# ScalarE's copy of U2 first in its pair, scaling of result rows in the pair's second place, result chunks made of runs of 32 elements

## The chip, the cores and the metric

The kernel runs on one core of a Trainium2 chip. A core has five engines that work side by side, each through its own instructions in order: TensorE (PE in the profile, its weight loads PEld), VectorE (DVE), ScalarE (ACT), GpSimd (POOL) and SyncE (SP, which here only issues transfers). They wait for one another through semaphores. SBUF is the working memory of 128 partitions, PSUM the memory into which TensorE writes and from which DVE and ACT read. The metric is the device time of one execution in microseconds (us), the median of several.

## What is computed

A block of attention, then a mixture of experts over 4096 tokens of 512 numbers:

```python
x = x + jnp.tanh(g_xattn[0]) * _L0_xattn_ref(_layernorm(x), ctx_1024, ctx_1024, ...)
x = x + jnp.tanh(g_ffn[0]) * _L0_ffn_ref(_layernorm(x), Wr, br, W1, b1, W2, b2)

# _L0_ffn_ref: 8 experts, 2 per token, each expert takes at most 615 rows
xg = x[disp_tok].reshape(E, cap, Dm)
h = jax.nn.silu(jnp.einsum('ecd,edh->ech', xg, W1) + b1[:, None, :])
out = jnp.einsum('ech,ehd->ecd', h, W2) + b2[:, None, :]
gated = out * disp_g.reshape(E, cap, 1)
y = jnp.zeros((N, Dm), x.dtype).at[disp_tok].add(gated.reshape(E * cap, Dm))
```

Each expert gathers its rows, multiplies them by W1 (512 x 2048), applies SiLU, multiplies by W2 (2048 x 512), scales each row by its gate and adds it to its token's row. All of it is in 32-bit floats.

## The kernel before

The first half of the time is attention, which the change doesn't touch. The experts follow one after another, with 616 columns (rows of the expert) in two halves of 308. Features lie on partitions: `xg_t` holds an expert's inputs, `o_t` its results, each as four chunks of 128 features.

**Products.** Both multiplications use Winograd's form of Strassen's scheme, with seven products in place of eight. `up(e, i)` (L912) computes pair i of an expert: hidden chunks i and i + 8 for both halves of the columns, 8 pairs per expert. Its products are of two matmuls each, and each matmul shows as two rows in the profile, so a product is four rows. In PE's order they are: P1, P2, U2 (added onto P1 in PSUM), P5, U3 (again onto P1), P3, and a last one onto P1. Between them stand small instructions: ACT copies P1 (`p1s`, L927), DVE adds it to P2 (`c11`, L930) and ACT applies SiLU (result "11", L931, recorded at L923); ACT copies U2 (L947), DVE adds P5 to it (`v`, L951); ACT copies U3 (L954), DVE makes c22 (L956), ACT SiLU "22"; DVE makes c12 (L961), ACT SiLU "12"; at last ACT applies SiLU "21" to PSUM itself. Since U3 is added onto the PSUM tile that holds U2, its matmuls wait for the copy of U2. `down` (L973) does the same for W2 in two long passes of eight matmuls a product.

**Weight and h sums.** The scheme needs sums of blocks. `sum_w1(e, i)` makes those of W1 on POOL, four instructions of 256 elements (L612 to L615). `sum_h(e, i)` makes those of the hidden results on DVE, four instructions of 308 elements (L880 to L883), each with two inputs in SBUF.

**What hangs on the pairs.** The order of all work is written out by hand. `up` calls `hook(1)` after SiLU "11" and `hook(3)` after SiLU "12"; `in_up` (L1124) says what they emit. At place 1 these are: in expert 0's pairs 2, 4 and 6 a step of the routing of later experts (`route_on`); the h sums of the pair before; the load of W1 three pairs ahead (SP); the weight sums of the next pair (POOL); from expert 1 on, in pairs 1 to 5, `put_laid` for a row chunk of the expert before, and in pairs 0 to 4 `lay_out` for one. At place 3 there is a routing step. A routing step is a string of small DVE instructions (L658 to L781) with a short matmul, or the gathers of an expert (L792, POOL).

**How results leave.** An expert's results are features by rows in `o_t` and must become rows. `lay_out(e, s)` (L827) transposes 32 x 32 blocks of a chunk of 128 rows on DVE into a tile `laid` (L832, or four pieces at L836 for the last chunk), and four transfers on SP (L840) bring its 32-partition pieces into a tile `eo` of 128 rows. `put_laid` (L856) scales the rows by their gates on ACT (L859) and issues, on POOL, an indirect transfer that adds the rows to the output (L1061). Three `eo` tiles take turns. Only the last expert's results go another way: `put_rows` (L1043) turns them on PE, scales them on ACT from PSUM (L1050) and scatters them.

**Layout of a row.** The weights come rearranged from the host (`chunks`, L1197): chunk c holds features 4 p + c on its partition p, for W1's inputs and for W2's outputs. So `lay_out` and `put_rows` put the four chunks side by side, element by element: a chunk's elements are written 16 bytes apart.

```python
# L830, lay_out; L1051, put_rows
to = t.rearrange("p (q i c) -> p q c i", q=DC, c=DC)
eo[:m, :].rearrange("p (i c) -> p c i", c=DC),
```

Of the kernel before, what the change touches and what calls it, by code (L numbers as in the profile page):

```python
# [17 lines left out]
P = 128  # L18
# [3 lines left out]
DC = D // P  # L22
TT = S // P
NT = B * TT
E, HID = 8, 2048
# [4 lines left out]
NST = 5  # L30
COLS = [min(P, C2 - s * P) for s in range(NST)]
BL = 32
# [12 lines left out]
def gated_block(ctx: ExitStack, tc: tile.TileContext, a: dict, out: bass.AP):  # L45
# [127 lines left out]
    with ExitStack() as at:  # L173
# [265 lines left out]
        for b in range(B):  # L439
            for c in range(DC):  # L440
                t = c * TT
# [36 lines left out]
        with tc.manual_schedule():  # L478
# [45 lines left out]
            for n, u in enumerate(units):  # L524
                b, c, qc = u
# [275 lines left out]

    laid, rows_out = {}, {}

    def lay_in(e, s):
# [20 lines left out]
    def lay_out(e, s):  # L827

        t = ex.tile([P, D], F32, tag="laid", name="laid", bufs=3)
        to = t.rearrange("p (q i c) -> p q c i", q=DC, c=DC)  # L830
        if LB[s] == BL:
            nc.vector.transpose(to, o_t[e][:, :, s * P : (s + 1) * P].rearrange("p c (q j) -> p q c j", q=DC))  # L832
        else:
            for q in range(DC):
                j0 = s * P + q * LB[s]
                nc.vector.transpose(to[:, q], o_t[e][:, :, j0 : j0 + BL])  # L836
        m = ROWS[s]
        rows_out[e, s] = ex.tile([P, D], F32, tag="eo", name="eo", bufs=3)
        for g in range(DC):
            nc.sync.dma_start(  # L840
                out=rows_out[e, s][:m, g * P : (g + 1) * P], in_=t[g * BL : g * BL + m // DC, :]
            )
# [13 lines left out]
    def put_laid(e, s):  # L856
        m = ROWS[s]
        eo = rows_out.pop((e, s))
        nc.scalar.activation(eo[:m, :], eo[:m, :], AF.Copy, scale=gates[e][:m, s : s + 1])  # L859
        put(e, s, eo, slots[:, e, :])  # L860
# [51 lines left out]
    def up(e, i, hook):  # L912

        w, s, x = w1.pop((e, i)), s1w.pop((e, i)), xg_t[e]
        k0, k1 = range(2), range(2, 4)
        if i == 0:
            h[e] = {}
        hh = h[e]

        def silu(q, g, src):  # L920
            hh[q, i] = ex.tile([P, CH], F32, tag=f"h{q}_{i}", name=f"h{q}_{i}")
            j = e * HC + i + g * NP
            nc.scalar.activation(hh[q, i], src, AF.Silu, bias=b1[:, j : j + 1])  # L923

        p1 = product([w[:, k, 0, :] for k in k0], [x[:, k, lhalf] for k in k0])
        p1s = temp("p1s")
        nc.scalar.copy(p1s, p1)  # L927
        p2 = product([w[:, k, 0, :] for k in k1], [x[:, k, lhalf] for k in k1])
        c11 = temp("c", 3)
        tt(c11, p2, p1s, ALU.add)  # L930
        silu("11", 0, c11)  # L931
        hook(1)
        first = e == 0 and i == 0

        def third():
            return product([s[:, 2, k, :] for k in k0], [x[:, k, rhalf] for k in k1])

        def fifth():
            return product([s[:, 0, k, :] for k in k0], [t[:, 0, k, :] for k in k0])

        t = tg[e]
        if first:

            p3, p5 = third(), fifth()
        product([s[:, 1, k, :] for k in k0], [t[:, 1, k, :] for k in k0], p1)
        u2 = temp("u2")
        nc.scalar.copy(u2, p1)  # L947
        if not first:
            p5 = fifth()
        v = temp("u4")  # L950
        tt(v, p5, u2, ALU.add)  # L951
        product([w[:, k, 1, :] for k in k0], [x[:, k, rhalf] for k in k0], p1)
        u3 = temp("u3")
        nc.scalar.copy(u3, p1)  # L954
        c22 = temp("c", 3)
        tt(c22, p5, u3, ALU.add)  # L956
        silu("22", 1, c22)
        if not first:
            p3 = third()
        c12 = temp("c", 3)  # L960
        tt(c12, p3, v, ALU.add)  # L961
        silu("12", 0, c12)
        hook(3)
        product([w[:, k, 1, :] for k in k1], [t[:, 2, k, :] for k in k0], p1)
        silu("21", 1, p1)
# [77 lines left out]
    def put_rows(e, s):  # L1043

        m = ROWS[s]
        pt = ps_x.tile([P, D], F32, tag="x", name="pt_o")
        for c in range(DC):
            nc.tensor.transpose(pt[:m, c * P : (c + 1) * P], o_t[e][:, c, s * P : s * P + m], ident)
        eo = ex.tile([P, D], F32, tag="eo", name="eo", bufs=3)
        nc.scalar.activation(  # L1050
            eo[:m, :].rearrange("p (i c) -> p c i", c=DC),  # L1051
            pt[:m, :].rearrange("p (c i) -> p c i", c=DC),
            AF.Copy,
            scale=last_gates[:m, s : s + 1],
        )
        put(e, s, eo, last_slots)
# [17 lines left out]
    with tc.manual_schedule():  # L1074
        load_w1(0, 0)
        load_w1(0, 1)
        for k, g in ((0, 1), (1, 1), (0, 0), (1, 0)):
            load_w2(0, 0, k, g, 1 + g)
        load_w1(0, 2)
        ex = ctx.enter_context(tc.tile_pool(name="ex", bufs=1))  # L1080
        candidates(0)
        for _ in range(BITS // LEVEL):
            narrow(0)
        above(0)
        places(0)
        one_hot(0, 0)
        for g in range(4):
            if g < 3:
                one_hot(0, g + 1)
            slot_tokens(0, g)  # L1090
        gather(0)

        idle = ps_h.tile([P, P], F32, tag="ps", name="idle")

        def busy(n):
            for _ in range(n):
                nc.tensor.matmul(idle, lhsT=ident, rhs=ident, start=True, stop=True)  # L1097

        busy(20)
        sum_w1(0, 0)  # L1100
        for s in range(3):
            turn(0, s)
            busy(4)

        def routing(e):

            yield lambda: candidates(e)
            for _ in range(BITS // LEVEL - 1):
                yield lambda: narrow(e)
            yield lambda: (narrow(e), above(e))  # L1110
            yield lambda: places(e)
            for g in range(4):
                yield lambda g=g: (one_hot(e, g), g and slot_tokens(e, g - 1))
            yield lambda: (slot_tokens(e, 3), gather(e))

        left = [step for e in range(1, E) for step in routing(e)]

        def route_on():
            if left:
                left.pop(0)()  # L1120

        for e in range(E):

            def in_up(i, n):  # L1124

                if n == 3:
                    if e == 0 or i > 1:
                        route_on()
                    return
                if e == 0 and i in (2, 4, 6):  # L1130
                    route_on()
                if i and i < NP:
                    sum_h(e, i - 1)
                if i + 3 < NP:
                    load_w1(e, i + 3)
                if 0 < i < NP - 1:
                    sum_w1(e, i + 1)
                if e:
                    if 0 < i <= NST:
                        put_laid(e - 1, i - 1)  # L1140
                    if i < NST:
                        lay_out(e - 1, i)
                if e == 0 and i == 0:

                    turn(0, 3)
                    turn(0, 4)
                    sum_x(0)
                    sum_w1(0, 1)
                if e == 0 and i == 5:
                    sum_w2(0, 0)  # L1150
                if e == E - 1 and i == NP - 1:
                    in_order(e)

            def in_down(m, n):
                if e == E - 1 and m == 1:
                    return
                if m == 0 and (n >= 0 if n % 1 == 0 else e == 0 and n < 0) or m == 1 and n in range(5):
                    route_on()
                if n % 1:
                    return  # L1160
                if m == 0 and n == 0:
                    sum_h(e, NP - 1)
                if e + 1 < E:
                    if m == 0 and n in (2, 4, 6):
                        load_w1(e + 1, n // 2 - 1)
                    if m == 0 and n == 6:
                        for s in range(3):
                            lay_in(e + 1, s)
                    if m == 1:
                        for s in ((0, 1), (2,), (3, 4), (), (), (), ())[n]:  # L1170
                            turn_laid(e + 1, s)
                        if n == 0:
                            lay_in(e + 1, 3)
                            lay_in(e + 1, 4)
                        if n == 3:
                            sum_x(e + 1)
                        if n in (1, 3):
                            sum_w1(e + 1, n // 2)

            for i in range(NP):  # L1180
                up(e, i, lambda n: in_up(i, n))
            for m in range(2):
                right_half = down(e, m, lambda n: in_down(m, n))
# [47 lines left out]
```

## Time and profile before

| What | us |
|---|---|
| median of 3 runs (2112.34 to 2114.98) | 2112.52 |
| the profiled execution | 2110.61 |
| its span, first to last instruction | 2108.5 |
| PE busy | 1999.0 (95%) |
| DVE busy | 1272.9 (60%) |
| ACT busy | 849.6 (40%) |
| POOL busy | 588.1 (28%) |
| attention, about | 0 to 1060 |
| experts, from expert 0's first product to the last product | 1120.6 to 2091.7 |

The granted TensorE clock is 0.986 on the mean. In the expert stage PE is busy for 98% of the time, DVE about 60%, ACT a quarter, POOL half; the transfers take up to half of the DMA engines' time.

How to read it: a row of a group gives line, engine, operation, the tiles written and read, their shape and the count; after the first bar the busy time in us and the mean of one in ns; after the second bar how long the engine had stood idle just before such instructions, and what ended that. A row of the timeline gives start and duration in us, then engine, line and operation; "x8" is eight rows of the same kind merged, and square brackets name an idle time before it. Matmuls are pipelined, so the end of one overlaps the start of the next; the pace of PE is read from starts. Waits of some 0.1 to 0.2 us are often not listed as waits, and are seen only in starts.

### The profile page before, as it was taken

How to read it: one execution, taken by the hardware profiler on the slowest of the kernel's cores; microseconds unless marked ns; L12 is line 12 of the kernel's file. 1: busy time of each engine (PE TensorE's matmuls, PEld its weight loads, DVE VectorE, ACT ScalarE, POOL GpSimd, SP SyncE). 2: the span in 40 equal slices, each digit the busy share in tenths (PEclk: the TensorE clock that was granted, in tenths of full speed). 3: DMA queues.
4: the chain of work that ended last, by engine and by line, in shares of the span. 5: the costliest groups of instructions: out<-in, count | busy, mean ns of one | idle time of the engine just before them, and what ended most of it. 6: DMA issues, size and time to landing. Idle time of an engine off the chain costs nothing.

```text
span 2108.5 us, 27762 instructions
## 1 busy us (share of the span) xinstructions
PE 1999.0 (95%) x9808; PEld 1237.5 (59%) x9808; DVE 1272.9 (60%) x2694; ACT 849.6 (40%) x2014; POOL 588.1 (28%) x800
## 2 busy tenths in 40 slices
PE   8999999999999999999749999999999999999997
PEld 3445555555555555555427667767777676767775
DVE  4566666566665666656576667676667667662430
ACT  3555556565555565655502214041322314042331
POOL 1001101010100001010104373554636354464623
PEclk9999999999999999999969999999999999999998
DMA  6010111002011010000042254555443444544431
GB/s 220 1 56 16 51 41 54 33 21 75 21 56 37 25 65 21 32 29 36 26 122 77 59 126 94 140 109 141 93 126 94 110 110 104 150 101 121 96 71 25
DMA packets 216938, 157.46 MB, mean 75 GB/s; under 512 B 17568, under 2 KB 186208, under 8 KB 216800
## 3 DMA queue, kind: packets, MB, share of 16 engines
q1 hardware_dynamic: 207968, 134.81, 21.7%
q0 software_dynamic: 8832, 20.88, 5.6%
q8 instruction: 78, 1.28, 0.3%
q14 instruction: 60, 0.49, 0.1%
HBM read 107.75 MB, written 29.77 MB: 65 GB/s over the span
## 4 chain that ended last, share of the span: by engine, by line
PE 89%; ACT 4%; DVE 3%; issue 2%; DMA 1%; POOL 0%; SPq 0%; POOLq 0%; DVEq 0%; ACTq 0%
PE ps L899 44%; PE pj L299 20%; PE pt L235 11%; PE s L340 6%; PE po L388 5%; ACT q_t L308 1%; ACT xn_t L268 1%; ACT xn_t L251 1%; ACT over L403 1%; PE pj_o L299 1%; DVE mask L667 0%; PE idle L1097 0%; PE s_o L299 0%; DMA wv<-in_Wv_t 0%; PE pl L276 0%
## 5 line engine op out<-in xcount | busy, mean ns | idle before, releaser
L356 ACT ACTIVATE pr<-s,nm 128x512 f32<-128x512 f32 x512 | 347.1, 704 | 2.5 <-DVE nm L349 2.5
L235 PEld LDWEIGHTS pt<-ident,pr 128*128 128x128 f32 x2048 | 225.0, 141 | 175.0 <-DVE p_t L410 78.1
L235 PE MATMUL pt<-ident,pr 128*128 128x128 f32 x2048 | 293.2, 279 | 34.1 <-ACT over L403 13.9
L349 DVE TENSOR_REDUCE nm<-s 128x2 f32<-128x1024 f32 x256 | 301.6, 1219 | 37.6 <-PE s L340 36.8
L407 ACT COPY p_t<-pt 128x512 f32<-128x512 f32 x256 | 137.5, 589 | 408.2 <-PE pt L235 408.2
L899 PE MATMUL ps<-xg_t,w 128*128 128x308 f32 x768 | 223.1, 426 | 7.6 <-issue 3.9
L222 POOL TENSOR_TENSOR rstd<-rstd,nhalf 128x1 f32<-128x1 f32 x64 | 37.2, 582 | 688.2 <-DVE rstd L221 688.2
L410 DVE COPY p_t<-pt 128x512 f32<-128x512 f32 x256 | 169.8, 687 | 70.5 <-PE pt L235 68.2
L899 PE MATMUL ps<-h,w 128*128 128x308 f32 x768 | 207.5, 425 | 0.0
L899 PEld LDWEIGHTS ps<-xg_t,w 128*128 128x128 f32 x768 | 142.5, 190 | 73.4 <-issue 24.8
L899 PEld LDWEIGHTS ps<-h,w 128*128 128x128 f32 x768 | 143.7, 190 | 52.6 <-issue 3.2
L340 PE MATMUL s<-k_t,q_t 32*128 32x512 f32 x1024 | 151.6, 643 | 2.9 <-ACT pr L356 2.0
L923 ACT ACTIVATE h<-c,b 128x308 f32<-128x308 f32 x192 | 104.2, 551 | 119.1 <-DVE c L930 79.4
L899 PE MATMUL ps<-tg,s1w 128*128 128x308 f32 x512 | 143.4, 423 | 1.4 <-ACT p1s L927 1.4
L404 DVE TENSOR_TENSOR o_t<-po,over 128x512 f32<-128x512 f32 x32 | 22.1, 692 | 191.9 <-ACT over L403 191.9
L899 PE MATMUL ps<-ht,s2w 128*128 128x308 f32 x512 | 137.9, 426 | 0.0
L299 PE MATMUL pj<-ctx_t,wk 128*128 128x512 f32 x256 | 117.3, 602 | 7.1 <-DMA ctx_t<-in_ctx_t 7.1
L388 PE MATMUL po<-p_t,v_s 128*32 128x512 f32 x1024 | 120.1, 602 | 0.0
L899 PEld LDWEIGHTS ps<-tg,s1w 128*128 128x128 f32 x512 | 96.7, 190 | 38.6 <-POOL o_t L978 1.9
L899 PEld LDWEIGHTS ps<-ht,s2w 128*128 128x128 f32 x512 | 95.5, 190 | 34.8 <-issue 1.8
L356 ACT ACTIVATION_READ_ACCUMULATOR pr<-s,nm 128x1 f32 x512 | 113.8, 222 | 0.0
L299 PE MATMUL pj<-xn_t,wq 128*128 128x512 f32 x248 | 111.6, 593 | 0.0
(192 smaller groups left out, 2903.2 us busy)
## 6 DMA issues: line engine op xcount, KB each, us to landing
w<-in_W SPq DMA_DIRECT2D x128, 256.0 KB
w<-in_W SPq DMA_DIRECT2D x64, 512.0 KB
x<-in_x SPq DMA_DIRECT2D x64, 256.0 KB
laid<-xg SPq DMA_DIRECT2D x140, 64.0 KB
out_x<-x SPq DMA_DIRECT2D x32, 256.0 KB
xn_rows<-xn SPq DMA_DIRECT2D x32, 256.0 KB
ctx_t<-in_ctx_t SPq DMA_DIRECT2D x7, 1024.0 KB
eo<-laid SPq DMA_DIRECT2D x112, 64.0 KB
```

The source lines that it names most:

```text
L222: nc.gpsimd.tensor_tensor(rstd, rstd, nhalf, ALU.pow)
L235: nc.tensor.transpose(pt[:, c, :], src[:, c * P : (c + 1) * P], ident)
L299: nc.tensor.matmul(ps, lhsT=lhs(ic), rhs=rhs(ic), start=(ic == 0), stop=(ic == DC - 1))
L340: nc.tensor.matmul(ps[i // 2][:, i % 2, :], lhsT=q_t[b, c][r, cols(qc)], rhs=k_t[b, c][r, :], start=True, stop=True,)
L349: nc.vector.tensor_reduce(nm[:, 2 * i : 2 * i + 2], ps[i], AX.X, ALU.max, negate=True)
L356: nc.scalar.activation(pr[:, i, :], ps[i // 2][:, i % 2, :], AF.Exp, bias=nm[:, i : i + 1], accum_out=sums[b, c][:, qc, i : i + 1],)
L388: nc.tensor.matmul(po[i * HD : (i + 1) * HD, :], lhsT=v_s[b][:, kc, h * HD : (h + 1) * HD], rhs=pts[i][:, kc, :], start=(kc == 0), stop=(k ...
L404: nc.vector.tensor_tensor(o_t[b][:, c, :], po, over, ALU.mult)
L407: nc.scalar.copy(dst, src)
L410: nc.vector.tensor_copy(dst, src)
L899: nc.tensor.matmul(ps, lhsT=lhs[k], rhs=rhs[k], start=(k == 0 and not onto), stop=(k == n - 1), skip_group_check=onto,)
L923: nc.scalar.activation(hh[q, i], src, AF.Silu, bias=b1[:, j : j + 1])
```

## The change

1. In `up`, the copy of U2 is emitted on ACT right after the U2 product; SiLU "11" and place 1 with all that hangs on it come after it, still ahead of P5. Only in the very first pair of expert 0 they stay where they were.
2. `put_laid` moves from place 1 to place 3, ahead of the routing step.
3. W2's output columns and b2 are rearranged in another way on the host: chunk c now holds, for each of four groups g of 128 features, the features 128 g + 32 c to 128 g + 32 c + 31, on partitions 32 g to 32 g + 31. So in `lay_out` and `put_rows` a chunk's elements are written in runs of 32 side by side. W1 keeps its order.

```diff
@@ lay_out
-        to = t.rearrange("p (q i c) -> p q c i", q=DC, c=DC)
+        to = t.rearrange("p (q c i) -> p q c i", q=DC, c=DC)
@@ up
         tt(c11, p2, p1s, ALU.add)
-        silu("11", 0, c11)
-        hook(1)
+
+        def go_on():
+            silu("11", 0, c11)
+            hook(1)
+
         first = e == 0 and i == 0
+        if first:
+            go_on()
...
         u2 = temp("u2")
         nc.scalar.copy(u2, p1)
         if not first:
+            go_on()
             p5 = fifth()
@@ put_rows
-            eo[:m, :].rearrange("p (i c) -> p c i", c=DC),
-            pt[:m, :].rearrange("p (c i) -> p c i", c=DC),
+            eo[:m, :].rearrange("p (g c i) -> p c g i", g=DC, c=DC),
+            pt[:m, :].rearrange("p (c g i) -> p c g i", g=DC, c=DC),
@@ in_up
                 if n == 3:
+                    if e and 0 < i <= NST:
+                        put_laid(e - 1, i - 1)
                     if e == 0 or i > 1:
                         route_on()
                     return
...
-                if e:
-                    if 0 < i <= NST:
-                        put_laid(e - 1, i - 1)
-                    if i < NST:
-                        lay_out(e - 1, i)
+                if e and i < NST:
+                    lay_out(e - 1, i)
@@ kernel
-    def chunks(v, axis):
+    def chunks(v, axis, *parts):
...
-        return v.reshape(*a, P, DC, *b).swapaxes(axis, axis + 1).reshape(v.shape)
+        return v.reshape(*a, *parts, *b).swapaxes(axis, axis + 1).reshape(v.shape)
...
-        "W1": chunks(g["W1"], 1),
+        "W1": chunks(g["W1"], 1, P, DC),
...
-        "W2": chunks(g["W2"], 2),
-        "b2_t": chunks(g["b2"], 1).reshape(E * DC, P).T,
+        "W2": chunks(g["W2"], 2, DC, DC, BL),
+        "b2_t": chunks(g["b2"], 1, DC, DC, BL).reshape(E * DC, P).T,
```

## The prediction

> **What bounds the kernel.** I read the page first: TensorE (PE) is 95% busy, the chain that ended last is 89% PE, and in the expert stage (from 1120 us) the slices are full.
>
> ```profile
> PE   8999999999999999999749999999999999999997
> ...
> PE 89%; ACT 4%; DVE 3%; issue 2%; DMA 1%; POOL 0%; SPq 0%; POOLq 0%; DVEq 0%; ACTq 0%
> ```
>
> So only what makes PE wait can move the time, and the groups (by shape) show small waits only. Third column: what the engine waited for.
>
> ```profile
> L1061 POOL DMA_INDIRECT out_x<-eo,slots x35 | 57.3, 1638 | 77.5 <-ACT eo L859 77.5
> ...
> L832 DVE STREAM_TRANSPOSE laid<-o_t 128x512 f32<-128x512 f32 x28 | 30.9, 1104 | 0.0
> ...
> L1050 ACT ACTIVATE eo<-pt_o,last_gates 128x512 f32<-128x512 f32 x4 | 4.4, 1160 | 4.7 <-PE pt_o L1048 3.0 <-DMA out_x<-eo,last_slots 1.6
> ```
>
> Then the timeline of one pair with scaling (expert 1, pair 2; start, duration):
>
> ```profile
> 1272.79 2.24 PE L899 MATMUL ps<-tg,s1w 128*128 128x308 f32 x8
> 1273.06 0.48 DVE L930 TENSOR_TENSOR c<-ps,p1s 128x308 f32<-128x308 f32 x1
> ...
> 1273.57 0.55 ACT L923 ACTIVATE h<-c,b 128x308 f32<-128x308 f32 x1 [1.15 <-DVE c L930]
> ...
> 1274.03 0.71 ACT L859 ACTIVATE eo<-eo,gates 128x512 f32<-128x512 f32 x1
> ...
> 1274.64 0.39 ACT L947 COPY u<-ps 128x308 f32<-128x308 f32 x1
> ...
> 1275.01 1.64 POOL L1061 DMA_INDIRECT out_x<-eo,slots  x1 [2.08 <-ACT eo L859]
> ...
> 1275.13 1.27 PE L899 MATMUL ps<-xg_t,w 128*128 128x308 f32 x4
> ```
>
> The first row is the U2 and P5 products. U2 is complete about 1.3 us after its start, but ScalarE first runs SiLU (0.55) and the scaling of a row chunk (0.71); the copy of U2 ends at 1275.03 and the U3 product starts at 1275.13. A pair without scaling shows the free pace:
>
> ```profile
> 1416.34 2.24 PE L899 MATMUL ps<-tg,s1w 128*128 128x308 f32 x8
> ...
> 1418.42 1.20 PE L899 MATMUL ps<-xg_t,w 128*128 128x308 f32 x4
> ```
>
> 2.08 us here against 2.34; and after the wait the U3 product holds its successor for 1.11 us instead of 1.04. That is 0.35 us per pair. Reading every pair so: 35 pairs scale (pairs 1 to 5 of experts 1 to 7). 29 lose 0.35, three 0.46 and three 1.19 (1650.08, 1763.69, 1877.19, where VectorE's routing work makes c11 late), 15.1 us together; one pair without scaling (1536.72) loses 0.58 for the same lateness.
>
> [...] at a place where POOL's weight sums meet the four h sums of L880 to L883:
>
> ```profile
> 1164.58 0.73 POOL L613 TENSOR_TENSOR s2w<-s2w,w 128x256 f32<-128x256 f32 x1
> 1164.83 0.82 DVE L880 TENSOR_TENSOR ht<-h,h 128x308 f32<-128x308 f32 x1
> ...
> 1165.27 0.96 POOL L614 TENSOR_TENSOR w<-w,w 128x256 f32<-128x256 f32 x1
> ...
> 1165.68 0.89 DVE L881 TENSOR_TENSOR ht<-h,ht 128x308 f32<-128x308 f32 x1
> ...
> 1166.19 0.96 POOL L615 TENSOR_TENSOR s2w<-w,s2w 128x256 f32<-128x256 f32 x1
> 1166.49 1.00 DVE L882 TENSOR_TENSOR h<-h,h 128x308 f32<-128x308 f32 x1
> ```
>
> They take turns: L880 to the next instruction (1168.33) is 3.50 us, against 1.68 (1273.45 to 1275.13) undisturbed. Transposes and sums with a PSUM input don't suffer (1.13 us for L832 at 1250.79 beside POOL's sums). [...] L859 (dense) shows 706, L1050 (every 16 bytes) 1160, so the spacing costs 0.45. [...] L832 shows 1104 ns, 387 for 128 elements (L836), so 1.87 ns per element[...].
>
> **U2 first.** In the 35 pairs the copy moves ahead of SiLU and scaling: it can run from 1.3 to 1.7, before P5's end at 2.07, as in the pair at 1416.34. All 15.1 + 0.6 = 15.7 us could go. SiLU "11" slips to about 1.7 to 2.2; its reader, the h sum, is a pair later, and the copy of U3 (about 3.4) is not delayed. With it moves the hook: the weight loads on SP, weight sums on POOL, and h sums and transposes on VectorE keep their order on each queue, and none waits for the copy. On PE the routing count of expert 0's even pairs now follows U2 (1.04 us later); VectorE's chain takes that at no cost in pairs 2 and 4 (p1s would be ready at 7.3, needed at 7.34), and pair 6 is bound by VectorE before and after. I take 0.5 us gained in expert 0.
>
> **Scaling to the second place.** On ScalarE it now stands between SiLU "12" and SiLU "21". Counting from the start of the U2 product, undisturbed: copy of U3 ends 3.8, c22 starts 3.82, and by the rows at 1178.90 to 1181.25 the two SiLUs, "21" and p1s follow so that U2 of the next pair can start 2.35 after c22, plus 0.61 for the scaling: 6.8, before PE's 7.25 (14 matmuls of 0.518; 7.34 with a routing count). No cost, with 0.5 to spare.
>
> But its scatter waits for it, and POOL works in order: behind it stands the next weight sum (L612 to L615). Before, the scatter was released at about 2.2 and was done when that sum's buffer came free at about 4.75. Now scaling ends at c22 + 2.11 = 5.9, the scatter starts 0.27 later and takes 1.64, and the sum starts at 7.86, that is 0.6 in the next pair: on top of the h sums, which start at 0.66. POOL's sum is needed a pair later (it would end near 4.6), so it costs PE nothing itself; VectorE is late. The row buffers (three) still have over 5 us before they are written again, and the loads behind them on SP are three pairs ahead.
>
> **Runs of 32.** L832 writes 32 elements in a row. Bounds: no gain (1.10)[...]. I take 0.68, since two engines show about the same cost for the spacing; 0.42 gained, hidden unless VectorE is late. Transfers keep their 2 KB and 512 B pieces, and the loads of W2 and b2 their shape. At the end L1050 falls from 1.16 to 0.71: the chain passes through one such instruction ahead of the first scatter, and the last scatter waits for a buffer that comes free that much earlier and for its own scaling: 2 x 0.45 = 0.9 us. Bounds 0 and 0.9.
>
> **The new wait, pair by pair** (experts 1 to 7). Four collisions end the h sums at 0.66 + 3.64 = 4.3 instead of 2.34, three at 3.9, two from an early start at 3.1.
> - Pair 1: its sum is not behind a scatter. No loss.
> - Pair 2: four collisions. Transpose 0.52 (spacing), v 0.39: c22 at 5.2, next U2 at 5.2 + 2.98 = 8.2, that is 0.85 over 7.34.
> - Pair 3: PE had waited, so c11 starts at -0.1 and the h sums at 0.28; two collisions, c22 at 4.0, U2 at 7.0. No loss.
> - Pair 4: three or four collisions, c22 4.8 to 5.2: 0.65 over.
> - Pairs 5 and 6: no transposes (pair 6 no scaling): c22 by 4.7, no loss.
> 1.5 us per expert, 10.5 in all, where the old order lost 15.7. The routing steps lose POOL as a neighbour (narrow: 1.83 without, 2.7 with), so the six late pairs end.
>
> **Sum**: -15.7 + 10.5 - 0.5 - 0.9 = -6.6 us. The profiled execution took 2110.61 (span 2108.5), giving 2104.0; the median of runs is 1.9 higher, so **2106**.
>
> **Rivals.**
> 1. No collision bites (the scatter's time shifts the sum past the h sums): -15.7 - 0.5 - 0.9 = -17.1, 2095. For: VectorE would need only 1 us less. Against: the sum's start, 0.6, falls right on the h sums.
> 2. The transpose stays at 1.10: pair 2 loses 1.27, pair 4 0.85, pair 3 0.05: 2.2 x 7 = 15.2; -1.9 in all, 2110.6. For: the transpose that reads every 16 bytes and writes densely (L819) has 1093, which would also fit a cost of its own.
> 3. Slower: VectorE's lateness. Transpose at 1.10 and four collisions in each of pairs 2, 3, 4: 3 x 1.27 = 3.8 per expert, 26.7: +9.6, 2122. It decides from 2.4 us per expert up ((15.7 + 1.4)/7). The early start of pair 3 speaks against it; pair 6 of expert 0, where PE waited 1.39 us for p1s after collisions, for it.
> 4. The order does nothing: 2112. The pair without scaling excludes it nearly.
>
> **Chances.** Forecast 0.45 (2102 to 2110), rivals 0.17, 0.23, 0.13 and 0.02. About 0.2% (4.2 us) is what a measurement of this kernel can tell: faster (under 2108.3) 0.36 + 0.17 + 0.05 = 0.58; same 0.09 + 0.16 + 0.02 = 0.27; slower 0.02 + 0.13 = 0.15. The range leaves out rival 3 and the lowest part of rival 1: 2094 to 2116.
>
> **What would show it.** The copy of U2 follows PE by 0.1 us, and U2 to U3 is 2.08 in pairs 1 to 5. L1061's wait for L859 grows; L612 starts after it, at 0.6 to 1.1 of the next pair; L880 to L883 grow from 0.47 toward 0.9; p1s L927 appears as PE's releaser in pairs 2 and 4. L832 near 0.68 and L1050 near 0.71. Wrong if L832 keeps 1.10, if PE waits for p1s in pair 3 too, or if the h sums stay at 0.47.

## The result, and the profile after

| | before | after |
|---|---|---|
| median of 22 runs each, us | 2111.22 (2108.87 to 2114.98) | 2107.81 (2104.67 to 2113.11) |
| ratio after to before | | 0.9985, 95% interval 0.9978 to 0.9991 |
| span of the profiled execution, us | 2108.5 | 2104.5 |

The gain is 3.2 us by the ratio, by the interval 1.9 to 4.6 (the medians differ by 3.4). So it is a real gain, but it lies under the 0.2% that the prediction took as its bound for "faster". The forecast was 6.6 us.

**What the change was to do, it did.** Three groups by shape of the kernel before, for comparison (its transposes, scatters and last scaling stand in the prediction):

```profile
L881 DVE TENSOR_TENSOR ht<-h,ht 128x308 f32<-128x308 f32 x64 | 31.5, 492 | 2.2
L882 DVE TENSOR_TENSOR h<-h,h 128x308 f32<-128x308 f32 x64 | 31.3, 489 | 0.0
...
L899 PE MATMUL ps<-tg,s1w 128*128 128x308 f32 x512 | 143.4, 423 | 1.4 <-ACT p1s L927 1.4
```

The groups of the kernel after (line numbers are 1 to 7 higher than before, so L881 and L882 are now L882 and L883):

```profile
L1068 POOL DMA_INDIRECT out_x<-eo,slots x35 | 55.6, 1589 | 116.7 <-ACT eo L860 66.9 <-DMA eo<-laid 49.8
L882 DVE TENSOR_TENSOR ht<-h,ht 128x308 f32<-128x308 f32 x64 | 52.6, 822 | 2.2
L883 DVE TENSOR_TENSOR h<-h,h 128x308 f32<-128x308 f32 x64 | 49.6, 776 | 0.0
L833 DVE STREAM_TRANSPOSE laid<-o_t 128x512 f32<-128x512 f32 x28 | 19.6, 700 | 0.0
L837 DVE STREAM_TRANSPOSE laid<-o_t 128x128 f32<-128x128 f32 x28 | 6.1, 272 | 0.0
L1057 ACT ACTIVATE eo<-pt_o,last_gates 128x512 f32<-128x512 f32 x4 | 2.6, 685 | 5.5 <-PE pt_o L1055 3.9 <-DMA out_x<-eo,last_slots 1.6
```

The transpose fell from 1104 to 700 ns (forecast 680) and the last scaling from 1160 to 685 (forecast 710). But these two h sums, 489 and 492 ns before, stand at 776 and 822, and POOL stands idle before the scatters for 116.7 us instead of 77.5. (The view puts 49.8 of it down to the transfer into `eo`; every one of the 35 scatters starts 0.27 to 0.37 us after the end of its scaling, before and after, so it is the scaling that releases them.) On the page, the PE group of the U2 products, which waited 1.4 us for p1s before, waits 9.3 for it, and the chain that ended last now runs through VectorE and ScalarE more than before (PE 89%, ACT 4%, DVE 3% then):

```profile
PE 81%; DVE 6%; ACT 5%; issue 3%; DMA 2%; SPq 2%; POOL 0%; POOLq 0%; ACTq 0%; DVEq 0%
...
L900 PE MATMUL ps<-tg,s1w 128*128 128x308 f32 x512 | 145.4, 426 | 9.3 <-ACT p1s L928 9.3
```

**Where it went back.** The timeline of the kernel after, from the end of expert 1's pair 2 to the start of its pair 4:

```profile
1271.73 0.70 ACT L860 ACTIVATE eo<-eo,gates 128x512 f32<-128x512 f32 x1
...
1272.71 1.56 POOL L1068 DMA_INDIRECT out_x<-eo,slots  x1 [2.71 <-DMA eo<-laid]
1272.74 0.40 ACT L928 COPY p1s<-ps 128x308 f32<-128x308 f32 x1
...
1273.28 2.31 PE L900 MATMUL ps<-tg,s1w 128*128 128x308 f32 x8 [0.29 <-ACT p1s L928]
1273.56 0.56 DVE L881 TENSOR_TENSOR ht<-h,h 128x308 f32<-128x308 f32 x1
1273.76 1.26 POOL L612 TENSOR_TENSOR s1w<-w 128x256 f32<-128x256 f32 x1
1274.16 1.22 DVE L882 TENSOR_TENSOR ht<-h,ht 128x308 f32<-128x308 f32 x1
1274.65 0.42 ACT L953 COPY u<-ps 128x308 f32<-128x308 f32 x1 [1.51 <-PE ps L900]
...
1275.11 0.86 POOL L613 TENSOR_TENSOR s1w<-s1w,w 128x256 f32<-128x256 f32 x1
1275.30 1.00 DVE L883 TENSOR_TENSOR h<-h,h 128x308 f32<-128x308 f32 x1
1275.43 1.20 PE L900 MATMUL ps<-xg_t,w 128*128 128x308 f32 x4
1275.92 0.96 POOL L614 TENSOR_TENSOR w<-w 128x256 f32<-128x256 f32 x1
1276.22 1.00 DVE L884 TENSOR_TENSOR ht<-h,ht 128x308 f32<-128x308 f32 x1
...
1277.14 0.70 DVE L833 STREAM_TRANSPOSE laid<-o_t 128x512 f32<-128x512 f32 x1
...
1278.13 0.45 DVE L963 TENSOR_TENSOR c<-ps,u 128x308 f32<-128x308 f32 x1
...
1280.53 0.40 ACT L928 COPY p1s<-ps 128x308 f32<-128x308 f32 x1
...
1281.07 2.31 PE L900 MATMUL ps<-tg,s1w 128*128 128x308 f32 x8 [0.19 <-ACT p1s L928]
```

The copy of U2 is out of PE's way: it ends at 1275.07, ahead of U3 (1275.43). But the scaling ends at 1272.43, the scatter starts 0.28 later and holds POOL; the record of the weight sum L612 behind it starts at 1273.76, in the middle of the h sums. From there VectorE and POOL take turns: L883, L884 and L833 start 0.92 us apart, where h sums alone start 0.4 to 0.5 apart. So c22 (L963) comes 4.85 after U2, p1s is late, and the pair takes 7.79 (1273.28 to 1281.07).

Reading all pairs so (starts of the U2 products), experts 1 to 7 on the mean: pair 1 went from 7.60 to 7.26, pair 5 from 7.90 to 7.49, but pairs 2, 3 and 4 from 7.69, 7.85 and 7.88 only to 7.83, 7.84 and 8.00.

### The profile page after: what moved, and what is told of

Read it like the earlier page. It is cut to its first block, busy times and chain, and to the rows that moved or that the text cites. A ratio compares the mean times of both kernels' runs of the same rounds, so it can differ in the third digit from the quotient of the medians.

```text
span 2104.5 us, 27762 instructions
## 1 busy us (share of the span) xinstructions
PE 1994.6 (95%) x9808; PEld 1238.7 (59%) x9808; DVE 1297.9 (62%) x2694; ACT 836.1 (40%) x2014; POOL 604.6 (29%) x800
## 4 chain that ended last, share of the span: by engine, by line
PE 81%; DVE 6%; ACT 5%; issue 3%; DMA 2%; SPq 2%; POOL 0%; POOLq 0%; ACTq 0%; DVEq 0%
PE ps L900 36%; PE pj L299 20%; PE pt L235 11%; PE s L340 7%; PE po L388 5%; DMA w<-in_W 2%; SPq L841 1%; DVE ht L884 1%; ACT q_t L308 1%; ACT xn_t L268 1%; ACT xn_t L251 1%; ACT over L403 1%; PE pj_o L299 1%; DVE mask L667 1%; ACT h L924 1%
```

## The experiments

The single profiles differ by up to 6 us in when expert 0's pair 1 starts (1132.56 to 1138.48), which is nearly all attention and routing that no kernel here touches. So each is read by three stretches from its timeline, which repeat from kernel to kernel within about 0.1 us (the end within 0.3): **expert 0**, from the U2 product of pair 1 to that of pair 7; **experts 1 to 7**, from the U2 product of expert 1's pair 0 to that of expert 7's pair 7; **the end**, from there to the end of the span. For the kernel after, the middle one is 2023.70 - 1250.86 = 772.84:

```profile
1250.86 0.94 PE L900 MATMUL ps<-tg,s1w 128*128 128x308 f32 x3
...
2023.70 1.20 PE L900 MATMUL ps<-tg,s1w 128*128 128x308 f32 x4
```

The change has three parts, and all eight combinations were measured, with two more kernels. Kernels 1 to 8 are those of the experiments below with these numbers; the stretches are in us.

| Kernel | U2 first | scaling second | runs of 32 | expert 0 | experts 1 to 7 | end | ratio to before (95%) |
|---|---|---|---|---|---|---|---|
| before | - | - | - | 47.64 | 776.99 | 81.39 | 1 |
| 5 | - | - | yes | 47.61 | 776.93 | 80.75 | 0.9996 (0.9987 to 1.0004) |
| 6 | yes | - | - | 48.18 | 761.31 | 81.34 | 0.9936 (0.9922 to 0.9949) |
| 7 | - | yes | - | 47.63 | 778.78 | 81.32 | 1.0009 (1.0001 to 1.0017) |
| 1 | yes | - | yes | 48.18 | 761.85 | 80.70 | 0.9928 (0.9915 to 0.9942) |
| 2 | - | yes | yes | 47.64 | 772.89 | 80.71 | 0.9981 (0.9973 to 0.9989) |
| 3 | yes | yes | - | 48.17 | 778.89 | 81.55 | 1.0015 (1.0008 to 1.0022) |
| after | yes | yes | yes | 48.18 | 772.84 | 80.80 | 0.9985 (0.9978 to 0.9991) |
| 4: after, weight sum ahead of the scaling | yes | yes | yes | 48.17 | 761.32 | 80.75 | 0.9920 (0.9906 to 0.9933) |
| 8: kernel 4, expert 0 in its old order | from expert 1 | yes | yes | 47.62 | 761.31 | 80.50 | 0.9923 (0.9910 to 0.9937) |

**1. The scaling back at place 1, the rest of the change kept.**

```diff
                 if n == 3:
-                    if e and 0 < i <= NST:
-                        put_laid(e - 1, i - 1)
...
-                if e and i < NST:
-                    lay_out(e - 1, i)
+                if e:
+                    if 0 < i <= NST:
+                        put_laid(e - 1, i - 1)
+                    if i < NST:
+                        lay_out(e - 1, i)
```

> The changed kernel with one part undone: scaling of a row chunk back at the first place of the pair (behind the copy of U2 and SiLU 11), U2 first and runs of 32 kept. Theory A (the late scatter holds POOL's next weight sum back until it falls on VectorE's h sums): the scatter is released at about 3.0 us of the pair and done by 4.9, the weight sum starts near 4.9 as it did in the kernel before, L881 to L884 are back at 0.47 us, every pair of experts 1 to 7 takes 7.25 to 7.35, and the time is about 16 us under that of before (2111 to 2095, ratio 0.9925). Rival B (the copy of U2 was never worth 0.35 us a pair, and the changed kernel gains only from its layout): about 3 us under, 0.9985 as the changed kernel.

Measured: 2096.85 us, ratio 0.9928. Pairs 2, 3 and 4 take 7.34, 7.37 and 7.39 on the mean, the h sums are back:

```profile
L882 DVE TENSOR_TENSOR ht<-h,ht 128x308 f32<-128x308 f32 x64 | 31.9, 498 | 2.2
L883 DVE TENSOR_TENSOR h<-h,h 128x308 f32<-128x308 f32 x64 | 31.3, 489 | 0.0
```

So the move of the scaling to the second place costs 11 us (772.84 - 761.85). The 0.54 over 761.31 come with one pair of 8.08 (from 1641.86): there the scaling, at the head of ScalarE's queue, waited 1.37 us for the transfer of its row chunk, and the copy of U3 stood behind it.

**2. The old order of U2, scaling second, runs of 32.**

```diff
-        if first:
-            go_on()
+        go_on()
...
         if not first:
-            go_on()
             p5 = fifth()
```

> The changed kernel with the order of U2 undone: SiLU 11 and the first place ahead of the copy of U2 again, scaling still in the second place, runs of 32 kept. Theory A: without the scaling in front, the copy follows SiLU at 1.3 us and is in time by itself, so U2 first adds nothing once scaling has moved: the same as the changed kernel, or 1 us less because expert 0's routing counts stand ahead of U2 again (ratio 0.998 to 0.9985). Rival C (U2 first is what removed the wait): 0.2 to 0.35 us a pair come back in 35 pairs, 7 to 12 us slower than the changed kernel, ratio 1.002 to 1.004.

Measured: 2109.01 us, ratio 0.9981. Experts 1 to 7 take 772.89, the same as after, with pairs 2, 3 and 4 at 7.83, 7.84 and 8.00 and U2 to U3 at 2.07 or 2.15, pair by pair as in the kernel after. Once the scaling is gone from place 1, SiLU "11" ahead of the copy costs PE nothing. The two parts of the change are two cures for one loss, and in experts 1 to 7 of the kernel after one of them does nothing; in expert 0 U2 first costs 0.54 us (48.18 against 47.64).

**3. The change without the runs of 32.**

```diff
-        to = t.rearrange("p (q c i) -> p q c i", q=DC, c=DC)
+        to = t.rearrange("p (q i c) -> p q c i", q=DC, c=DC)
```

(and `put_rows`, W2 and b2 likewise).

> The changed kernel with the layout undone (elements of a chunk 16 bytes apart in lay_out and put_rows, W2 and b2 arranged as before), order of the kernel after kept. Theory A: VectorE sets the pace in pairs 2 to 4, so the transpose at 1.10 instead of 0.70 costs up to 0.4 in each of 21 pairs, and the end 0.6: 6 to 9 us slower than the changed kernel, ratio to the kernel before 1.0015 to 1.003. Rival D (VectorE's transposes are hidden): only the end, 0.6 us, ratio 0.9988.

Measured: 2115.6 us, ratio 1.0015. The transposes are long again, and PE's waits for p1s (the view of PE's waits in the expert stage) grow from 9.3 to 15.2 us:

```profile
L833 DVE STREAM_TRANSPOSE laid<-o_t 128x512 f32<-128x512 f32 x28 | 30.9, 1104 | 0.0
```

```profile
PE ps L900 <- ACT p1s L928: 15.2, 23, 2.3
```

The pairs 2, 3 and 4 are at 8.17, 8.19 and 8.16. With the scaling second, the layout is worth 6.05 us in experts 1 to 7 (778.89 - 772.84), and without it the change is slower than before by 0.15% (0.08 to 0.22).

**4. The weight sum issued ahead of the scaling.** The scaling and the copy of U2 stay where the change put them; from expert 1 on, the weight sums of the pair after next go in front of the scatter on POOL, at place 3.

```diff
                 if n == 3:
+                    if e and 0 < i < NP - 2:
+                        sum_w1(e, i + 2)
                     if e and 0 < i <= NST:
                         put_laid(e - 1, i - 1)
...
-                if 0 < i < NP - 1:
+                if 0 < i < NP - 1 and (e == 0 or i == 1):
                     sum_w1(e, i + 1)
```

> The changed kernel with one thing more: POOL's weight sum of the pair after next is issued in the second place ahead of the scaling and its scatter, not behind it in the next pair's first place. Scaling stays in the second place on ScalarE. Theory A: POOL's sum runs at about 4.4 to 7.5 as in the kernel before, the h sums are undisturbed, no wait for p1s in experts 1 to 7: 12 to 13 us less than the changed kernel, ratio 0.9925 to 0.993. Rival E (what costs the 1.65 us per expert is scaling itself, 0.6 us of ScalarE ahead of SiLU 21 and p1s): the waits for p1s stay, ratio 0.998 to 0.9985 as the changed kernel.

Measured: 2094.86 us, ratio 0.9920, experts 1 to 7 at 761.32. The timeline, expert 1, from the end of pair 2 into pair 3:

```profile
1276.85 0.70 ACT L860 ACTIVATE eo<-eo,gates 128x512 f32<-128x512 f32 x1
...
1278.13 0.92 POOL L615 TENSOR_TENSOR s1w<-w,s1w 128x256 f32<-128x256 f32 x1
...
1278.90 2.24 PE L900 MATMUL ps<-tg,s1w 128*128 128x308 f32 x8
...
1279.21 1.56 POOL L1068 DMA_INDIRECT out_x<-eo,slots  x1 [0.16 <-issue]
1279.57 0.47 DVE L881 TENSOR_TENSOR ht<-h,h 128x308 f32<-128x308 f32 x1
1280.07 0.48 DVE L882 TENSOR_TENSOR ht<-h,ht 128x308 f32<-128x308 f32 x1
...
1280.47 0.47 DVE L883 TENSOR_TENSOR h<-h,h 128x308 f32<-128x308 f32 x1
...
1281.25 0.70 DVE L833 STREAM_TRANSPOSE laid<-o_t 128x512 f32<-128x512 f32 x1
```

The weight sum ends at 1279.05, before the first h sum (1279.57); now the scatter stands behind it and starts 1.66 us after the end of its scaling. The h sums are undisturbed, though the scaling is still second on ScalarE. So the loss does not come about without the order on POOL's queue: the 0.7 us of scaling on ScalarE alone cost nothing (761.32 against 761.31 in kernel 6). They still count once c22 is late: from c22 to the next U2 pair 2 of the kernel after takes 2.95 us, and the prediction read 2.35 for a pair without scaling. With c22 at 4.88 that would give a U2 at 7.23, which is not late; this is an estimate from these two figures. Pair 6 of the kernel after, which has the late sum but neither scaling nor transposes, loses nothing (7.44, as in kernel 6); no run has the late sum and the transposes without the scaling. It also shows that the scatter itself does not hold VectorE up: it runs from 1279.21 to 1280.77, beside h sums of 0.47 to 0.48.

**5. The runs of 32 alone, in the old order.** The edits of kernels 1 and 2 together.

> The old order in full, and only the runs of 32. Theory (the layout shortens L832 to 0.70 us and L1050 to 0.69 us, and with the old order VectorE isn't late, so only the end gains): pairs 2 to 5 still 7.60 to 7.75 with U2 to U3 at 2.34, the end 0.6 us shorter, about 2110.5 against 2111.2, ratio 0.9997. Rival (the layout has a gain of its own in the old order, for instance in the six late pairs, where the transposes stand ahead of c11): 3 us or more, ratio under 0.9986.

Measured: 2111.42 us, ratio 0.9996; 776.93 against 776.99, the end 0.64 shorter. In the old order the 11 us that the shorter transposes save on VectorE (28 of 0.40) buy nothing for PE, since VectorE had time to spare.

**6. U2 first alone.** The edits of kernels 1 and 3 together.

> U2 first alone: scaling stays at place 1 but behind the copy, layout as before. Theory (what the old order lost was the copy of U2 behind the scaling, 15 us, and nothing collides while the scaling is at place 1): U2 to U3 at 2.07 in all pairs, h sums 0.47 to 0.50 us, pairs of experts 1 to 7 at 7.25 and 7.37, ratio 0.993. Rival (transposes of 1.10 us need the shorter layout once the pairs run at 7.25): pairs 2 to 4 at 7.5 or more, ratio over 0.996.

Measured: 2098.04 us, ratio 0.9936. Experts 1 to 7 take 761.31, 15.68 less than before. The transposes of 1.1 us don't matter here: kernel 1, with the short ones, is no faster. The h sums are undisturbed and U2 is copied in time:

```profile
1267.41 0.47 DVE L881 TENSOR_TENSOR ht<-h,h 128x308 f32<-128x308 f32 x1
...
1268.04 0.41 ACT L953 COPY u<-ps 128x308 f32<-128x308 f32 x1 [1.66 <-PE ps L900]
```

**7. The scaling second alone.** The edits of kernels 2 and 3 together.

> Only the scaling moved to the second place; U2 stays behind SiLU "11", layout as before. Theory (with the scaling gone from place 1, SiLU alone delays the copy of U2 by nothing; the pairs 2 to 4 collide as with the old layout): U2 to U3 at 2.07, pairs 2 to 4 at about 8.15, ratio 1.001, the same within 0.002 as with U2 first in the old layout. Rival (the copy behind SiLU makes the collisions worse): U2 to U3 over 2.2 in pairs 2 to 4, pairs over 8.3, ratio over 1.003.

Measured: 2113.1 us, ratio 1.0009, pairs 2, 3 and 4 at 8.17, 8.19 and 8.16. U2 to U3 is 2.07 in pairs 1 and 2 but 2.15 in pairs 3 to 5, a little more than the theory said. The place of the copy is not the reason: kernel 3 and the kernel after, with U2 first, show the same 2.15 in the same pairs. These are the pairs whose U2 product had to wait for p1s, and after such a wait its eight rows take 2.31 us in place of 2.24. So it costs nothing on top: with U2 first the stretch is 778.89, without it 778.78.

**8. The weight sum ahead, and expert 0 in its old order.** Kernel 4, with this:

```diff
-        if first:
+        if e == 0:
             go_on()
...
         if not first:
-            go_on()
+            if e:
+                go_on()
             p5 = fifth()
```

> The kernel with the weight sum ahead of the scaling, with expert 0's pairs in their old order as well (SiLU "11" and place 1 ahead of the copy of U2). Theory (in expert 0 the routing count behind U2 is what makes VectorE late): expert 0's stretch from pair 1 to pair 7 falls from 48.2 to about 47.6 us, PE's wait for p1s there from about 2.7 to 1.4 us, the whole 0.5 to 1.0 us under the kernel with the sum ahead, ratio about 0.9915. Rival (the count's place doesn't matter, the stretch of 48.2 is noise): stretch 48.2 again and no difference.

Measured: 2094.45 us, ratio 0.9923. The view of PE's waits in the expert stage:

```profile
PE ps L900 <- ACT p1s L928: 1.4, 1, 1.4
```

In kernel 4 it was 2.7 us in two waits. Expert 0's stretch falls from 48.17 to 47.62, as the theory said. The whole can't be told from kernel 4 (the intervals of both are 0.0027 wide); the 0.55 us are shown by the stretch alone. Both kernels are faster than the one before and the one after.

## Why the prediction was right in part, and where it failed

In the three stretches the profile after gains 4.15 + 0.59 - 0.54 = 4.2 us, where 6.6 were forecast; the ratio of the runs gives 1.9 to 4.6. By the forecast's terms (the sums are of unrounded figures):

| Step | forecast | measured | from |
|---|---|---|---|
| U2 first, experts 1 to 7 | -15.7 | -15.7 | 761.31 (kernel 6) against 776.99 (before) |
| the new wait, experts 1 to 7 | +10.5 | +11.5 | 772.84 (after) against 761.31 (kernel 6) |
| expert 0 | -0.5 | +0.5 | 48.18 against 47.64 |
| the end | -0.9 | -0.6 | 80.80 against 81.39 |
| sum | -6.6 | -4.2 | |

- **U2 first**: right, in size too. The kernel with U2 first alone shows it. The late pairs with routing are gone in that kernel as well, though POOL's weight sum stands there where it did (4.40 after U2); so it was not the loss of POOL as a neighbour that ended them.
- **The new wait**: the mechanism is the forecast one (scaling late, scatter late, weight sum behind it on the h sums), and kernels 1 and 4 show it by taking it away in two ways. What failed is the count of collisions in each pair, and the sum came near (10.5 for 11.5) in part by luck, as the errors of pairs 2 and 3 cancel. Pair 2 was to meet four collisions and lose 0.85; it met three, with the first h sum of the pair nearly free (0.54 us), and lost 0.49 (7.83 against 7.34 in the kernel with U2 first alone). The 3.64 us that were put down for four collisions are also more than the 3.50 that the prediction had read. Pair 3 was to lose nothing, with two collisions and c22 at 4.0 because its h sums start early; it lost 0.47 (7.84 against 7.37), with three collisions and c22 at 4.85. So PE waits for p1s after pair 3 too, which the prediction had named as a sign that it was wrong. Pair 4 lost 0.61 for a forecast 0.65, pair 5 0.07 for none, pair 6 none as forecast. In pair 3 the h sums do start at 0.28, as forecast. The forecast let the weight sum start when the scatter's 1.64 us are over. In the timeline above the scatter's record ends 0.99 after U2, but that of L612 starts at 0.48 already, and L612 takes its turn ahead of the second h sum (L882, from 0.88, 1.22 us long), not behind it. How POOL's queue gets there ahead of the scatter's end is not shown. The rest of that step held: from c22 to the next U2 2.95 in pair 2 (2.98 forecast).
- **Expert 0**: wrong in sign. Pairs 1 to 4 did gain 0.40: 1134.05 to 1163.75 is 29.70, against 1133.61 to 1163.71, 30.10. Pair 6 was called "bound by VectorE before and after", and so it is, but the step took the start of that chain of VectorE as given. In pair 4 the routing count now runs 1.04 after U2, where it ran 0.10 ahead of it; VectorE waits 0.24 for it, and the pair's h sums start 2.83 after U2 instead of 2.32. VectorE has no idle time after that to make it up, and in pair 6 c11 comes at 1173.29 instead of 1172.14. From pair 5's U2 to pair 7's it is 18.48 against 17.54, and PE's last wait for p1s there is 2.34 instead of 1.39. Kernel 8, which puts the count and the rest of place 1 ahead of the copy again in expert 0, takes it back.
- **Runs of 32**: the times of both instructions came near the forecast (700 ns for 680, 685 for 710), and the layout did nothing where VectorE had time (kernel 5, 776.93 against 776.99). The 680 was the author's estimate: the trace of before showed the cost of the spacing on ScalarE only (1160 against 706 ns), since no transpose there was without it (1104 where it writes with the spacing, 1093 where it reads with it). That two engines show about the same cost is seen in the runs of after: 404 ns on VectorE (1104 - 700), 475 on ScalarE (1160 - 685). Rival 2, a transpose that stays at 1.10, is kernel 3: 778.89 - 761.31 = 17.6 us lost, 2.5 per expert against its 2.2. Had the layout not helped, the change would have been 0.15% slower than before, in rival 3's direction but a third of its size. Rival 1 (no collision) is excluded by the h sums of 776 to 822 ns, rival 4 (the order does nothing) by kernel 6.
- **The end**: 0.6 in place of 0.9; it is shorter in all kernels with the layout (80.50 to 80.80 against 81.32 to 81.55 without). The last scatter did start earlier by 1.23 us, counted from the last U2 (71.56 against 72.79), but from there to the end of the span it took 0.64 longer (9.24 against 8.60). Why is open.

The prediction gave 0.58 to a gain of more than 0.2%, and the measured 0.15% falls on the other side of that bound. Two steps of about 1 us each, the new wait and expert 0, make most of the difference to the forecast.

## What to carry to other kernels

When an instruction is moved back on one engine, look at what it releases on an in-order queue, and at what stands behind that: here 0.7 us of ScalarE work, moved to a place where it cost nothing by itself, delayed a scatter, and the scatter delayed an unrelated sum into a collision with VectorE. Where two edits may cure the same wait, measure each alone, and keep the one that costs the other queues less; here U2 first alone gains 13 us, and scaling second alone nothing. If a late item must stay, put the work that has a due time ahead of it in the queue, as kernel 4 does (experts 1 to 7 at 761.32, against 772.84 after).

## What the runs showed of the hardware

- In the kernel before, VectorE's sums of two SBUF inputs (128 x 308) follow one another at 0.39 to 0.51 us when alone (1273.45 to 1275.13), POOL's sums (128 x 256) at 0.68 to 0.82 (1250.62 to 1252.81). Where they meet they take turns, one of each every 0.92 us (the kernel after, 1275.30 to 1277.14), which is less than both paces added (at least 1.07).
- Beside POOL's sums, VectorE's transposes into `laid` (128 x 512) and its sums with a PSUM input kept their times: by medians over the expert stage, the transposes took 1.12 us beside and 1.10 alone before, 0.70 in both cases after; the sums (L930, L951, L956, L961 of before) 0.47 to 0.48 in both cases.
- The indirect scatter on POOL (1.56 us) ran beside VectorE's sums without lengthening them (kernel 4, 0.47 to 0.48 us each); what was held up in the kernel after is the sum behind it in POOL's queue.
- A 32-bit transpose on VectorE cost, from the 128 and 512 element forms (L836 and L832 before, L837 and L833 after), (1104 - 387) / 384 = 1.87 ns an element when it writes every 16 bytes, and (700 - 272) / 384 = 1.11 when it writes 32 elements in a row. On ScalarE, the same spacing cost 1160 - 685 = 475 ns for 512 elements (L1050 before, L1057 after).
